# A two-layer graph network on one core: zeroing beside the sort, the search in the sort's buffers, layer norm beside the gathers

## The chip, the cores and the metric

The kernel runs on one core of a Trainium2 chip. The metric is the device time of one execution in microseconds (us). Engines are named as in the profile: PE (TensorE; PEld its weight loads), DVE (VectorE), ACT (ScalarE), POOL (GpSimd) and SP (SyncE). SP and ACT issue hardware DMAs, POOL issues the indirect ones (gathers by an index table).

## The reference

```python
h = jnp.maximum(_layernorm(x), 0.0)            # x: 12500 nodes x 48
x = x + _L0_gnn_ref(h, edge_index, W, b)       # edge_index = [src, dst], 400000 edges, dst sorted
h = jnp.maximum(_layernorm(x), 0.0)
x = x + _L1_gnn_ref(h, edge_index, edge_attr_16, W1, b1, W2, b2, W3, b3)
```

`_L0` adds up, for each `src` node, the rows of its `dst` nodes, scaled by the degrees, and multiplies by a 48 x 48 matrix. `_L1` runs a three-layer perceptron (112 to 128 to 128 to 48) over every edge, averages the messages by `dst` node and adds them to `x`.

## The kernel before, in words

There are three stages. The **preparation** (up to L642) brings the edge lists into the form that layer 0 needs. **Layer 0** (L645 to L852) works on it with one-hot matmuls. **Layer 1** (L906 to L1000) gathers one 128-edge tile after the other (L937) and runs the perceptron on it; its result is added into two tables `utab` in HBM, which must have been zeroed before. Only the preparation is changed.

The preparation runs in this order of the source:

- L106 loads the `dst` list as 71 partitions of 22,528 bytes (`raw`), L155 loads `x`, L160 to L177 the weights and biases. SP and ACT share them.
- L223 to L230 reduce `raw` to a maximum per 128 edges and put it into a table `rtab`; L252 reads it back for all partitions into `ka`. From it, 112 partitions each look for their own stretch of 4096 edges and gather it (L264, L277, L287: `mix_i`, `run_i`).
- L306 to L312 reduce `raw` to `lim` and write a table `wtab`. L314 to L330 turn `raw` into edge-major form: ACT converts (L322, `rawf`), PE transposes (L329), ACT evicts (L330). This is done for `dst` (into `rel`) and then, with a second load (L317), for `src` (into `src_i`).
- L286 to L301 make one sort key for each edge. L332 to L354 are a bitonic sort of 4096 keys in each of 112 partitions: 78 stages of two or four DVE instructions that go from buffer `ka` to `kb` and back. L356 writes the sorted keys to HBM (`ltab`), L357 keeps a sample of every 64th.
- L359 zeroes `utab`: a memset of `zero` (L198) and 14 DMAs of 128 x 1806 floats on SP's queue (L203).
- L400 to L412 search the sample for the place of 50 limits in each run (`coarse`, `where_i`). L414 gathers, for each limit, the 64 keys around it (`fine`, 50 gathers on POOL). L418 to L451 read `wtab` back (`wb2`, `top2`) and use it.
- L460 to L474 are the first layer norm and the 48 x 48 product: `norm_relu` (L362 to L383) in two halves, then 25 blocks of up to four tiles. For each block PE transposes (L468, `tp`), ACT evicts (L470), PE multiplies (L473, `lin`), ACT evicts (L474).
- L476 to L492 count in `fine`, give the exact slots, and end in the flag `good`, for which PE does one small matmul (L490, `w_ps`). Every engine reads `good` and branches on it (L642, L645).

Layer 0 then begins with 49 gathers of sorted keys (`slots`, L656); PE transposes them four at a time (L664), DVE and ACT work on them (L666 to L718).

The order in which an engine meets its instructions is not that of the source: a scheduler of the framework orders all instructions by its own estimate, and puts a wait where a buffer is written or read. Within one engine the order is then fixed. Buffers come from pools that are opened and closed like a stack; a tile in space that an earlier pool used waits for whoever used it last. DMAs of SP and ACT take eight hardware semaphores in turn, and a DMA waits until the one eight places before it has landed.

Of the kernel before, what the change touches and what calls it, by code (L numbers as in the profile page):

```python
# [15 lines left out]
P = 128  # L16
# [4 lines left out]
def kernel(  # L21
# [45 lines left out]
    B = 4  # L67
# [34 lines left out]

    early = ExitStack()
# [90 lines left out]
    def clear(tables, w, engines):  # L194

        with tc.tile_pool(name="zero", bufs=1) as zp:
            zero = zp.tile([P, ZH * w], FP, name="zero")
            nc.vector.memset(zero, 0.0)  # L198
            for k, t in enumerate(tables):
                v = t.rearrange("(p h) f -> p (h f)", p=P)  # L200
                n, m = v.shape[1], ZH * w
                for a in range(0, n, m):
                    engines[k % len(engines)].dma_start(  # L203
                        v[:, a : min(a + m, n)], zero[:, : min(m, n - a)]
                    )
# [32 lines left out]
    with tc.tile_pool(name="runs", bufs=1) as rp, tc.tile_pool(  # L238
        name="runs_ps", bufs=2, space=bass.MemoryType.PSUM
    ) as eps:  # L240
        iota_si = rp.tile([P, S], I32, name="iota_si")
        nc.gpsimd.iota(iota_si, pattern=[[1, S]], base=0, channel_multiplier=0)
        nc.vector.tensor_copy(iota_s, iota_si)
        run_i = rp.tile([ND, RUN], I32, name="run_i")
        nc.gpsimd.iota(run_i, pattern=[[1, RUN]], base=0, channel_multiplier=0)
        at = rp.tile([ND, RUN], FP, name="at")
        nc.vector.tensor_copy(at, run_i)
        ka = rp.tile([ND, RUN + P], FP, name="ka")
        kb = rp.tile([ND, RUN], FP, name="kb")
        nc.vector.memset(ka[:, RUN:], BIG)  # L250
        rmax, below = ka[:, :NT], kb[:, :NT]
        nc.sync.dma_start(rmax, rtab[0:1, :].to_broadcast([ND, NT]))  # L252
        ends2 = rp.tile([ND, 2], FP, name="ends2")
        for k in range(2):
            lim = rp.tile([ND, 1], FP, name=f"lim{k}")
            nc.vector.tensor_scalar(lim, first, float(k * D), None, op0=OP.add)
            nc.vector.tensor_scalar(below, rmax, lim, None, op0=OP.is_lt)
            whole = rp.tile([ND, 1], FP, name=f"whole{k}")
            nc.vector.tensor_reduce(whole, below, AX.X, OP.add)
            nc.vector.tensor_scalar(whole, whole, float(NT - 1), None, op0=OP.min)  # L260
            whole_i = rp.tile([ND, 1], I32, name=f"whole_i{k}")
            nc.vector.tensor_copy(whole_i, whole)
            mix_i = rp.tile([ND, P], I32, name=f"mix_i{k}")
            gather(mix_i, dst.rearrange("(t p) -> t p", p=P), whole_i)  # L264
            mix_f = rp.tile([ND, P], FP, name=f"mix_f{k}")
            nc.vector.tensor_copy(mix_f, mix_i)
            nc.vector.tensor_scalar(mix_f, mix_f, lim, None, op0=OP.is_lt)
            part = rp.tile([ND, 1], FP, name=f"part{k}")
            nc.vector.tensor_reduce(part, mix_f, AX.X, OP.add)
            nc.vector.scalar_tensor_tensor(  # L270
                ends2[:, k : k + 1], whole, float(P), part, op0=OP.mult, op1=OP.add
            )
        base = rp.tile([ND, 1], FP, name="base")
        nc.vector.tensor_scalar(base, ends2[:, 0:1], float(E - RUN), None, op0=OP.min)
        base_i = rp.tile([ND, 1], I32, name="base_i")
        nc.vector.tensor_copy(base_i, base)
        gather(run_i, dst.rearrange("(e o) -> e o", o=1), base_i)  # L277
        offs = rp.tile([ND, 2], FP, name="offs")
        nc.vector.tensor_scalar(offs, ends2, base, None, op0=OP.subtract)


        nc.vector.tensor_scalar(kb, at, offs[:, 0:1], None, op0=OP.is_ge)
        nc.vector.scalar_tensor_tensor(at, at, offs[:, 1:2], kb, op0=OP.is_lt, op1=OP.mult)
        inside = at
        sa, sb = ka[:, :RUN], kb
        nc.vector.tensor_scalar(sa, run_i, first, None, op0=OP.subtract)  # L286
        gather(run_i, src.rearrange("(e o) -> e o", o=1), base_i)  # L287
        nc.vector.tensor_tensor(kb, sa, inside, OP.mult)
        nc.vector.tensor_reduce(wrong[:, 0:1], kb, AX.X, OP.max)
        nc.vector.tensor_scalar(  # L290
            wrong[:, 0:1], wrong[:, 0:1], D - 0.5, None, op0=OP.is_gt
        )
        nc.vector.tensor_reduce(wrong[:, 1:2], kb, AX.X, OP.min)
        nc.vector.tensor_scalar(wrong[:, 1:2], wrong[:, 1:2], -0.5, None, op0=OP.is_lt)
        nc.vector.tensor_scalar(wrong[:, 2:3], offs[:, 1:2], RUN + 0.5, None, op0=OP.is_gt)
        nc.vector.tensor_tensor(wrong[:, 3:4], offs[:, 0:1], offs[:, 1:2], OP.is_gt)
        nc.vector.scalar_tensor_tensor(sa, run_i, float(P), sa, op0=OP.mult, op1=OP.add)
        nc.vector.scalar_tensor_tensor(
            sa, sa, BIG, inside, op0=OP.subtract, op1=OP.mult
        )  # L300
        nc.vector.tensor_scalar(sa, sa, BIG, None, op0=OP.add)  # L301


        lim = ep.tile([CP, 2, CC], FP, name="lim")
        flat = raw_d.rearrange("p (c e) -> p c e", c=CC)
        nc.vector.tensor_reduce(lim[:, 0], flat, AX.X, OP.min)  # L306
        nc.vector.tensor_reduce(lim[:, 1], flat, AX.X, OP.max)
        for k in range(2):
            nc.sync.dma_start(
                wtab[k, :NCH].rearrange("(p c) -> p c", p=CP), lim[:, k]  # L310
            )
            nc.sync.dma_start(wtab[k : k + 1, NCH:], lim1[:, k : k + 1])  # L312
        raw = raw_d
        for k, o in ((1, rel), (0, src_i)):  # L314
            if k == 0:
                raw = ep.tile([CP, CC * B * P], I32, name="raw")
                nc.sync.dma_start(raw, src[:E4].rearrange("(p e) -> p e", p=CP))  # L317
            nc.scalar.activation(o[:, NCH * B :], last_i[:, k : k + 1], AF.Copy)
            ov = o[:, : NCH * B].rearrange("p (q c b) -> p c q b", q=CP, b=B)
            for c in range(CC):  # L320
                rawf = ep.tile([CP, P, B], FP, name="rawf", bufs=3)
                nc.scalar.activation(  # L322
                    rawf,
                    raw.rearrange("p (c i j) -> p c i j", c=CC, j=B)[:, c],
                    AF.Copy,
                )
                tp = eps.tile([P, B, CP], FP, name="tp")
                for b in range(B):
                    nc.tensor.transpose(tp[:, b, :], rawf[:, :, b], ident[:CP, :CP])  # L329
                nc.scalar.activation(ov[:, c], tp.rearrange("p b q -> p q b"), AF.Copy)  # L330

        k = 2  # L332
        while k <= RUN:
            j = k // 2
            while j >= 1:
                if k < RUN:
                    a = sa.rearrange("p (n d m h j) -> p n d m h j", d=2, m=k // (2 * j), h=2, j=j)
                    b = sb.rearrange("p (n d m h j) -> p n d m h j", d=2, m=k // (2 * j), h=2, j=j)
                    ways = [(a[:, :, d], b[:, :, d], d) for d in range(2)]
                else:  # L340
                    a = sa.rearrange("p (n m h j) -> p n m h j", n=1, h=2, j=j)
                    b = sb.rearrange("p (n m h j) -> p n m h j", n=1, h=2, j=j)
                    ways = [(a, b, 0)]
                for a, b, d in ways:
                    for h in range(2):
                        nc.vector.tensor_tensor(  # L346
                            b[:, :, :, h],
                            a[:, :, :, 0],
                            a[:, :, :, 1],
                            OP.max if h != d else OP.min,  # L350
                        )
                sa, sb = sb, sa
                j //= 2
            k *= 2  # L354
        assert sa.offset == ka.offset
        nc.sync.dma_start(ltab, ka)  # L356
        nc.vector.tensor_copy(sample, sa.rearrange("p (i k) -> p i k", k=SK)[:, :, 0])  # L357
# [38 lines left out]
    with tc.tile_pool(name="begin", bufs=1) as bp_, tc.tile_pool(  # L396
# [59 lines left out]
        with tc.tile_pool(name="ln0", bufs=2) as lp, tc.tile_pool(  # L456
# [5 lines left out]
            for h0 in range(0, NH, HC):  # L462
                at_once(norm_relu(lp, h0, h0 + HC))
# [674 lines left out]
```

## Time and profile before

| | us |
|---|---|
| median of 4 runs (lowest to highest) | 6191.4 (6187.16 to 6197.04) |
| the profiled execution, its own time | 6189.63 |
| its span, first to last instruction | 6187.9 |
| DVE from the first to the last stage of the sort | 204.64 to 564.28 |
| flag `good` written (L492, start) | 692.91 |
| first gather of layer 0 (L656, `slots`) | 694.99 |

All starts are counted from the first instruction of the span. A row of the timeline reads: start, duration, engine, line, operation, written tile, read tiles, shape, count, and in brackets the idle time before it with what ended it. "SPq" and "ACTq" are the queues' DMA issues: the duration is that of the issue and not of the transfer. A row of the waits reads: who waited on whose instruction, us in total, times, longest.

### The profile page before, as it was taken

The numbers are of one execution on the slowest core, as the hardware profiler recorded it, in microseconds if no ns is written. First come the engines' busy times: TensorE is split into PE (matmuls) and PEld (weight loads), VectorE is DVE, ScalarE is ACT, GpSimd is POOL, SyncE is SP. The second block draws the span as 40 slices with busy tenths as digits, with TensorE's granted clock in tenths as the row PEclk, the third lists the DMA queues.
The fourth block names the chain that finished last, engine by engine and source line by source line (L and its number), as shares of the span: only waits on it lengthen the run. The fifth ranks groups of instructions, "written<-read, shape, count | busy, mean of one in ns | idle before, by whom it ended". The sixth has DMA issues, their size and how long they took to land.

```text
span 6187.9 us, 97254 instructions
## 1 busy us (share of the span) xinstructions
PE 4425.6 (72%) x35368; PEld 3350.1 (54%) x35368; DVE 3163.4 (51%) x4843; ACT 2302.3 (37%) x4904; POOL 3179.9 (51%) x3239
## 2 busy tenths in 40 slices
PE   0001559999999777777777777777777777777776
PEld 0001449999999555555455555455555555555555
DVE  3898489999999433333333333333333333333333
ACT  0001228888888422232223232333323223223331
POOL 0000700000000577777777777777777777777771
PEclk9999869999999899999999999999999999999996
DMA  2002134455444222222222222222222222222224
GB/s 69 3 0 99 31 82 149 146 148 146 147 147 144 63 48 47 47 44 48 48 46 48 44 48 46 48 44 48 48 46 47 45 48 46 47 44 48 46 40 105
DMA packets 397108, 407.58 MB, mean 66 GB/s; under 512 B 227482, under 2 KB 350958, under 8 KB 392111
## 3 DMA queue, kind: packets, MB, share of 16 engines
q1 hardware_dynamic: 155238, 273.99, 15.9%
q0 software_dynamic: 103488, 85.03, 10.1%
q10 hardware_dynamic: 137894, 42.24, 2.9%
q8 instruction: 283, 4.64, 0.3%
q14 instruction: 205, 1.67, 0.1%
HBM read 362.97 MB, written 38.02 MB: 65 GB/s over the span
## 4 chain that ended last, share of the span: by engine, by line
DMA 29%; PE 21%; POOL 17%; DVE 14%; issue 10%; ACT 6%; another core or an unknown queue 2%; POOLq 0%; ACTq 0%; DVEq 0%
DMA et<-htab,src_i 29%; POOL et L208 16%; PE u_ps L990 6%; ACT rows L797 5%; PE h_ps L970 3%; PE sum L809 3%; DVE kb L346 3%; DVE ka L346 3%; PE et_ps L953 2%; DVE ohs L781 2%; PE at_ps L793 2%; PE h_ps L959 2%; DVE oht L777 1%; DVE ohr L695 1%
## 5 line engine op out<-in xcount | busy, mean ns | idle before, releaser
L208 POOL DMA_INDIRECT et<-htab,src_i x3125 | 3055.6, 978 | 2230.6 <-PE tb L636 1277.4
L953 PE MATMUL et_ps<-ident,et 128*64 128x128 f32 x3125 | 686.1, 287 | 948.6 <-DMA et<-htab,src_i 936.2
L953 PEld LDWEIGHTS et_ps<-ident,et 128*64 128x64 f32 x3125 | 347.5, 111 | 1673.6 <-DMA et<-htab,src_i 985.8
L963 ACT ACTIVATE h<-h_ps,b_sb 128x512 f32<-128x512 f32 x782 | 537.7, 688 | 1623.7 <-PE h_ps L959 1623.7
L809 PE MATMUL sum<-rows,ohs 128*128 128x144 bf16 x10976 | 1008.8, 228 | 20.3 <-ACT rows L797 17.3
L797 ACT ACTIVATE rows<-at_ps 128x432 bf16<-128x432 f32 x1830 | 955.3, 531 | 142.9 <-DVE g L756 35.1
L974 DVE MEMSET h<- 128x4 f32 x782 | 48.5, 62 | 1844.4 <-PE u_ps L990 1844.4
L970 PE MATMUL h_ps<-w_sb,h 128*128 128x128 f32 x6250 | 990.0, 306 | 0.5 <-ACT h L963 0.5
L970 PEld LDWEIGHTS h_ps<-w_sb,h 128*128 128x128 f32 x6250 | 835.6, 208 | 170.8 <-ACT et L934 131.6
L990 PE MATMUL u_ps<-h,oh 128*40 128x129 f32 x6250 | 915.8, 292 | 0.0
L809 PEld LDWEIGHTS <-ohs 128*128 128x128 bf16 x10976 | 855.8, 144 | 25.7 <-issue 19.4
L975 DVE TENSOR_TENSOR h<-h_ps,b_neg 128x512 f32<-128x512 f32 x782 | 540.4, 691 | 594.5 <-PE h_ps L970 594.5
L959 PE MATMUL h_ps<-mv,wk 104*128 104x512 f32 x1564 | 828.3, 612 | 0.0
L954 ACT ACTIVATE mv<-et_ps 64x512 f32<-64x512 f32 x782 | 460.0, 588 | 988.6 <-PE et_ps L953 987.8
L781 DVE TENSOR_TENSOR ohs<-lo_b,iota_x 128x4096 bf16<-128x4096 bf16 (+1 forms) x350 | 786.0, 2246 | 51.1 <-PE sum L809 32.8
L990 PEld LDWEIGHTS u_ps<-h,oh 128*40 128x40 f32 x6250 | 679.8, 122 | 122.6 <-issue 33.2
L793 PE MATMUL at_ps<-g,oht 112*128 112x144 bf16 x5488 | 651.3, 226 | 35.9 <-DVE oht L777 35.5
L596 DVE TENSOR_SCALAR mv<-db,wid 40x512 f32<-40x512 int32 x782 | 534.1, 683 | 185.0 <-PE h_ps L959 174.6
L793 PEld LDWEIGHTS <-oht 112*128 112x128 bf16 x5488 | 416.2, 98 | 38.9 <-issue 35.9
L468 PE MATMUL tp<-ident,ht 128*48 128x128 f32 x98 | 25.7, 415 | 415.1 <-ACT ht L383 415.1
L208 POOL DMA_INDIRECT fine<-ltab,where_i x50 | 46.7, 934 | 506.3 <-ACT h_t L470 491.4
L941 DVE TENSOR_TENSOR oh<-rel,iota_f 128x160 f32<-128x160 f32 x782 | 255.7, 327 | 13.3 <-DMA wk<-in_L_gnn_W_dram 2.8
(190 smaller groups left out, 2382.3 us busy)
## 6 DMA issues: line engine op xcount, KB each, us to landing
at<-dltab SPq DMA_DIRECT2D x343, 448.0 KB
db<-in_dst_dram SPq DMA_DIRECT2D x97, 640.0 KB
et<-htab,src_i POOLq DMA_INDIRECT x3125, 2.5
ea<-in_edge_attr_dram ACTq DMA_DIRECT2D x97, 256.0 KB
utab<-zero SPq DMA_DIRECT2D x14, 903.0 KB
utab<-u SPq DMA_DIRECT2D x391, 20.2 KB
wk<-btab SPq DMA_DIRECT2D x391, 20.0 KB
uk<-utab SPq DMA_DIRECT2D x7, 903.0 KB
```

Source lines behind the costliest of these rows:

```text
L208: nc.gpsimd.indirect_dma_start(out=into, out_offset=None, in_=table, in_offset=bass.IndirectOffsetOnAxis(ap=idx, axis=0),)
L596: nc.vector.tensor_scalar(to.rearrange("p (j i) -> p j i", j=n), db[p0 : p0 + W, a : a + n * P].rearrange("p (i j) -> p j i", j=n), wid[p0 ...
L781: nc.vector.tensor_tensor(ohs[:, :n], lo_b[:, h0 : h0 + n, None, c : c + CG].to_broadcast([P, n, S, CG]), iota_x[:, None].to_broadcast([P, ...
L793: nc.tensor.matmul(ps3[:, i, :], oht[:, k, c % CG, :], g3[:, c, :], start=True, stop=True)
L797: nc.scalar.activation(rows[:, : len(tiles)], ps3[:, : len(tiles)], AF.Copy)
L809: nc.tensor.matmul(sums[k][:, j, :], ohs[:, k, j * P : (j + 1) * P, c % CG], rows[:, i, :], start=(c == 0 and j == 0), stop=(c == ND - 1 a ...
L953: nc.tensor.transpose(et_ps[:, j * P : (j + 1) * P], et[:, j, :], ident)
L959: nc.tensor.matmul(h1_ps[:, : n * P], k["wc"], k["mv"][:, : n * P], start=True, stop=True)
L963: nc.scalar.activation(h1[:, : n * P], h1_ps[:, : n * P], AF.Relu, bias=b1_sb)
L970: nc.tensor.matmul(h2_ps[:, j, :], h1[:, j * P : (j + 1) * P], w2_sb, start=True, stop=True)
L975: nc.vector.tensor_tensor(h2[:, :n, :H], h2_ps[:, :n], b2_neg[:, None, :].to_broadcast([P, n, H]), OP.max,)
L990: nc.tensor.matmul(u_ps, oh[:, j, :], h2[:, j, :], start=(q == 0 and j == 0), stop=(q == Q - 1 and j == n - 1),)
```

## The change

The sort's pool (`runs`) is opened earlier and stays open until `good` is written, so that its buffers can be used again. `clear` takes a pool from outside and is called before the sort in the source. `coarse` and `fine` become one view of the sort's buffer `at`; `wb2` and `top2` become views of `ka`; the layer norm's work space becomes the two halves of `kb`, which for that is declared as 128 x 2 x 2499 floats, of which the sort uses the first 4096 of 112 partitions. No operation is added or left out.

```diff
+    cut = ExitStack()
+    rp = cut.enter_context(tc.tile_pool(name="cuts", bufs=1))
+    where_i = rp.tile([ND, 2, NS + 1], I32, name="where_i")
+    sorting = ExitStack()
+    rp = sorting.enter_context(tc.tile_pool(name="runs", bufs=1))
     early = ExitStack()
...
-    def clear(tables, w, engines):
+    def clear(tables, w, engines, pool):
-        with tc.tile_pool(name="zero", bufs=1) as zp:
-            zero = zp.tile([P, ZH * w], FP, name="zero")
+        zero = pool.tile([P, ZH * w], FP, name="zero")
...
-        ka = rp.tile([ND, RUN + P], FP, name="ka")
-        kb = rp.tile([ND, RUN], FP, name="kb")
+    ka_all = rp.tile([P, RUN + P], FP, name="ka")
+    ka = ka_all[:ND]
+    HC = NH // 2
+    kb_all = rp.tile([P, 2, (F + 3) * HC], FP, name="kb")
+    kb = kb_all[:ND].rearrange("p k n -> p (k n)")[:, :RUN]
...
+    clear(utab, H1, (nc.sync, nc.sync), rp)
+
         k = 2
         while k <= RUN:
...
-    clear(utab, H1, (nc.sync, nc.sync))
     early.close()
-    def norm_relu(pool, h0, h1):
+    def norm_relu(pool, h0, h1, space=None):
+        if space is None:
             st = pool.tile([P, 3, n], FP, name="st")
             sq = pool.tile([P, n, F], FP, name="sq")
+        else:
+            st = space[:, : 3 * n].rearrange("p (k n) -> p k n", k=3)
+            sq = space[:, 3 * n :].rearrange("p (n f) -> p n f", f=F)
...
-        coarse = bp_.tile([ND, NS1, NK], FP, name="coarse")
+        coarse = fine = at[:, : NS1 * NK].rearrange("p (h k) -> p h k", k=NK)
...
-        fine = bp_.tile([ND, NS1, SK], FP, name="fine")
...
-        wb2 = bp_.tile([P, NG, Q], FP, name="wb2")
+        wb2 = ka_all[:, :NC1].rearrange("p (g q) -> p g q", q=Q)
...
-        top2 = bp_.tile([1, NG, Q], FP, name="top2")
+        top2 = ka_all[:1, NC1 : 2 * NC1].rearrange("p (g q) -> p g q", q=Q)
...
-            for h0 in range(0, NH, HC):
-                at_once(norm_relu(lp, h0, h0 + HC))
+            for k in range(2):
+                at_once(norm_relu(lp, k * HC, (k + 1) * HC, kb_all[:, k]))
...
+    sorting.close()
```

More of the change, by code (lines that the diff above doesn't have):

```diff
@@ L192 @@
     ZH = 14
-    def clear(tables, w, engines):
-        with tc.tile_pool(name="zero", bufs=1) as zp:
-            zero = zp.tile([P, ZH * w], FP, name="zero")
[L198 to L205, printed above, removed]
+    def clear(tables, w, engines, pool):
+        zero = pool.tile([P, ZH * w], FP, name="zero")
+        nc.vector.memset(zero, 0.0)
+        for k, t in enumerate(tables):
+            v = t.rearrange("(p h) f -> p (h f)", p=P)
+            n, m = v.shape[1], ZH * w
+            for a in range(0, n, m):
+                engines[k % len(engines)].dma_start(
+                    v[:, a : min(a + m, n)], zero[:, : min(m, n - a)]
+                )
     def gather(into, table, idx):
@@ L237 @@
     wrong = const.tile([ND, 5], FP, name="wrong")
[L238 to L247, printed above, removed]
-        ka = rp.tile([ND, RUN + P], FP, name="ka")
-        kb = rp.tile([ND, RUN], FP, name="kb")
[L250 to L271, printed above, removed]
-            )
[L273 to L357, printed above, removed]
@@ L359 @@
-    clear(utab, H1, (nc.sync, nc.sync))
+    eps = early.enter_context(tc.tile_pool(name="runs_ps", bufs=2, space=bass.MemoryType.PSUM))
+    iota_si = rp.tile([P, S], I32, name="iota_si")
+    nc.gpsimd.iota(iota_si, pattern=[[1, S]], base=0, channel_multiplier=0)
+    nc.vector.tensor_copy(iota_s, iota_si)
+    run_i = rp.tile([ND, RUN], I32, name="run_i")
+    nc.gpsimd.iota(run_i, pattern=[[1, RUN]], base=0, channel_multiplier=0)
+    at = rp.tile([ND, RUN], FP, name="at")
+    nc.vector.tensor_copy(at, run_i)
@@ new lines @@
+    ka_all = rp.tile([P, RUN + P], FP, name="ka")
[3 more added lines that the diff above has]
+    kb = kb_all[:ND].rearrange("p k n -> p (k n)")[:, :RUN]
+    nc.vector.memset(ka[:, RUN:], BIG)
+    rmax, below = ka[:, :NT], kb[:, :NT]
+    nc.sync.dma_start(rmax, rtab[0:1, :].to_broadcast([ND, NT]))
+    ends2 = rp.tile([ND, 2], FP, name="ends2")
+    for k in range(2):
+        lim = rp.tile([ND, 1], FP, name=f"lim{k}")
+        nc.vector.tensor_scalar(lim, first, float(k * D), None, op0=OP.add)
+        nc.vector.tensor_scalar(below, rmax, lim, None, op0=OP.is_lt)
+        whole = rp.tile([ND, 1], FP, name=f"whole{k}")
+        nc.vector.tensor_reduce(whole, below, AX.X, OP.add)
+        nc.vector.tensor_scalar(whole, whole, float(NT - 1), None, op0=OP.min)
+        whole_i = rp.tile([ND, 1], I32, name=f"whole_i{k}")
+        nc.vector.tensor_copy(whole_i, whole)
+        mix_i = rp.tile([ND, P], I32, name=f"mix_i{k}")
+        gather(mix_i, dst.rearrange("(t p) -> t p", p=P), whole_i)
+        mix_f = rp.tile([ND, P], FP, name=f"mix_f{k}")
+        nc.vector.tensor_copy(mix_f, mix_i)
+        nc.vector.tensor_scalar(mix_f, mix_f, lim, None, op0=OP.is_lt)
+        part = rp.tile([ND, 1], FP, name=f"part{k}")
+        nc.vector.tensor_reduce(part, mix_f, AX.X, OP.add)
+        nc.vector.scalar_tensor_tensor(
+            ends2[:, k : k + 1], whole, float(P), part, op0=OP.mult, op1=OP.add
+        )
@@ new lines @@
+    base = rp.tile([ND, 1], FP, name="base")
+    nc.vector.tensor_scalar(base, ends2[:, 0:1], float(E - RUN), None, op0=OP.min)
+    base_i = rp.tile([ND, 1], I32, name="base_i")
+    nc.vector.tensor_copy(base_i, base)
+    gather(run_i, dst.rearrange("(e o) -> e o", o=1), base_i)
+    offs = rp.tile([ND, 2], FP, name="offs")
+    nc.vector.tensor_scalar(offs, ends2, base, None, op0=OP.subtract)
+    nc.vector.tensor_scalar(kb, at, offs[:, 0:1], None, op0=OP.is_ge)
+    nc.vector.scalar_tensor_tensor(at, at, offs[:, 1:2], kb, op0=OP.is_lt, op1=OP.mult)
@@ new lines @@
+    inside = at
+    sa, sb = ka[:, :RUN], kb
+    nc.vector.tensor_scalar(sa, run_i, first, None, op0=OP.subtract)
+    gather(run_i, src.rearrange("(e o) -> e o", o=1), base_i)
+    nc.vector.tensor_tensor(kb, sa, inside, OP.mult)
+    nc.vector.tensor_reduce(wrong[:, 0:1], kb, AX.X, OP.max)
+    nc.vector.tensor_scalar(
+        wrong[:, 0:1], wrong[:, 0:1], D - 0.5, None, op0=OP.is_gt
+    )
+    nc.vector.tensor_reduce(wrong[:, 1:2], kb, AX.X, OP.min)
+    nc.vector.tensor_scalar(wrong[:, 1:2], wrong[:, 1:2], -0.5, None, op0=OP.is_lt)
@@ new lines @@
+    nc.vector.tensor_scalar(wrong[:, 2:3], offs[:, 1:2], RUN + 0.5, None, op0=OP.is_gt)
+    nc.vector.tensor_tensor(wrong[:, 3:4], offs[:, 0:1], offs[:, 1:2], OP.is_gt)
+    nc.vector.scalar_tensor_tensor(sa, run_i, float(P), sa, op0=OP.mult, op1=OP.add)
+    nc.vector.scalar_tensor_tensor(
+        sa, sa, BIG, inside, op0=OP.subtract, op1=OP.mult
+    )
+    nc.vector.tensor_scalar(sa, sa, BIG, None, op0=OP.add)
+    lim = ep.tile([CP, 2, CC], FP, name="lim")
+    flat = raw_d.rearrange("p (c e) -> p c e", c=CC)
@@ new lines @@
+    nc.vector.tensor_reduce(lim[:, 0], flat, AX.X, OP.min)
+    nc.vector.tensor_reduce(lim[:, 1], flat, AX.X, OP.max)
+    for k in range(2):
+        nc.sync.dma_start(
+            wtab[k, :NCH].rearrange("(p c) -> p c", p=CP), lim[:, k]
+        )
+        nc.sync.dma_start(wtab[k : k + 1, NCH:], lim1[:, k : k + 1])
+    raw = raw_d
+    for k, o in ((1, rel), (0, src_i)):
+        if k == 0:
+            raw = ep.tile([CP, CC * B * P], I32, name="raw")
+            nc.sync.dma_start(raw, src[:E4].rearrange("(p e) -> p e", p=CP))
+        nc.scalar.activation(o[:, NCH * B :], last_i[:, k : k + 1], AF.Copy)
+        ov = o[:, : NCH * B].rearrange("p (q c b) -> p c q b", q=CP, b=B)
+        for c in range(CC):
+            rawf = ep.tile([CP, P, B], FP, name="rawf", bufs=3)
+            nc.scalar.activation(
+                rawf,
+                raw.rearrange("p (c i j) -> p c i j", c=CC, j=B)[:, c],
+                AF.Copy,
+            )
+            tp = eps.tile([P, B, CP], FP, name="tp")
+            for b in range(B):
+                nc.tensor.transpose(tp[:, b, :], rawf[:, :, b], ident[:CP, :CP])
+            nc.scalar.activation(ov[:, c], tp.rearrange("p b q -> p q b"), AF.Copy)
@@ new lines @@
+    clear(utab, H1, (nc.sync, nc.sync), rp)
+    k = 2
+    while k <= RUN:
+        j = k // 2
+        while j >= 1:
+            if k < RUN:
+                a = sa.rearrange("p (n d m h j) -> p n d m h j", d=2, m=k // (2 * j), h=2, j=j)
+                b = sb.rearrange("p (n d m h j) -> p n d m h j", d=2, m=k // (2 * j), h=2, j=j)
+                ways = [(a[:, :, d], b[:, :, d], d) for d in range(2)]
+            else:
+                a = sa.rearrange("p (n m h j) -> p n m h j", n=1, h=2, j=j)
+                b = sb.rearrange("p (n m h j) -> p n m h j", n=1, h=2, j=j)
+                ways = [(a, b, 0)]
+            for a, b, d in ways:
+                for h in range(2):
+                    nc.vector.tensor_tensor(
+                        b[:, :, :, h],
+                        a[:, :, :, 0],
+                        a[:, :, :, 1],
+                        OP.max if h != d else OP.min,
+                    )
+            sa, sb = sb, sa
+            j //= 2
+        k *= 2
@@ L360 @@
+    assert sa.offset == ka.offset
+    nc.sync.dma_start(ltab, ka)
+    nc.vector.tensor_copy(sample, sa.rearrange("p (i k) -> p i k", k=SK)[:, :, 0])
     early.close()
-    def norm_relu(pool, h0, h1):
+    def norm_relu(pool, h0, h1, space=None):
         n = h1 - h0
         xs, hs = xt[:, h0:h1, :], ht[:, h0:h1, :]
-        st = pool.tile([P, 3, n], FP, name="st")
-        sq = pool.tile([P, n, F], FP, name="sq")
+        if space is None:
+            st = pool.tile([P, 3, n], FP, name="st")
+            sq = pool.tile([P, n, F], FP, name="sq")
+        else:
+            st = space[:, : 3 * n].rearrange("p (k n) -> p k n", k=3)
+            sq = space[:, 3 * n :].rearrange("p (n f) -> p n f", f=F)
@@ L387, in at_once @@
             pass
-    cut = ExitStack()
-    rp = cut.enter_context(tc.tile_pool(name="cuts", bufs=1))
     lflat = ltab.rearrange("p e -> (p e)").rearrange("(e o) -> e o", o=1)
@@ L394 @@
     NS1 = NS + 1
-    where_i = rp.tile([ND, 2, NS1], I32, name="where_i")
     with tc.tile_pool(name="begin", bufs=1) as bp_, tc.tile_pool(
@@ L451 @@
         nc.vector.tensor_reduce(worst, bad.rearrange("p a b -> p (a b)"), AX.X, OP.max)
-        HC = NH // 2
         w0_t = const.tile([F, F], FP, name="w0_t")
@@ L461 @@
             nc.vector.tensor_copy(w0_t, wt_ps)
-            for h0 in range(0, NH, HC):
-                at_once(norm_relu(lp, h0, h0 + HC))
+            for k in range(2):
+                at_once(norm_relu(lp, k * HC, (k + 1) * HC, kb_all[:, k]))
             for h0 in range(0, NH, B):
@@ L880 @@
         scaled()
-        clear([acc0], F, (nc.sync,))
-        clear([acc1], F1, (nc.sync,))
+        with tc.tile_pool(name="zero", bufs=1) as zp:
+            clear([acc0], F, (nc.sync,), zp)
+        with tc.tile_pool(name="zero", bufs=1) as zp:
+            clear([acc1], F1, (nc.sync,), zp)
         with tc.tile_pool(name="s0", bufs=2) as wp, tc.tile_pool(
```

## The prediction

> **What bounds the kernel now.** I read first the program's order on each engine before and after the change, with what each instruction waits for, to find how far the change reaches. From the first gather of layer 0 (`slots`) on, every engine has the same instructions in the same order, with the same waits, DMA semaphores and buffer addresses. So only the preparation counts, the first 695 us of the span, and there the time from its start to the first `slots` gather. The costliest group of the whole page (3125 gathers in layer 1) is out of reach.
>
> The preparation has three parts with different bounds. Ahead of the sort, the waits between 60 and 210 us show (who waited on whom: total, times, longest):
>
> ```profile
> ACT rawf L322 <- DMA raw<-in_src_dram: 79.3, 1, 79.3
> DVE w_t L461 <- PE wt_ps L460: 51.8, 1, 51.8
> ```
>
> ACT waits 79.3 us for the `src` list, a load of 71 long partitions. PE transposes it, and `wt_ps` (L460) stands behind those transposes on PE; DVE waits 51.8 us for it and only then starts the sort. So the landing of the `src` list starts the sort, and everything else ahead of it has about 50 us of slack. In the sort DVE is alone and its instructions follow each other; it bounds itself. Behind the sort, the waits between 560 and 700 us:
>
> ```profile
> DVE fine L476 <- DMA fine<-ltab,where_i: 60.4, 1, 60.4
> ...
> PEld w_ps L490 <- DVE wsum L488: 25.7, 1, 25.7
> PE w_ps L490 <- DVE wsum L488: 25.6, 1, 25.6
> ...
> DVE coarse L400 <- DMA utab<-zero: 11.9, 1, 11.9
> ...
> DVE zero L198 <- DMA ltab<-ka: 8.1, 1, 8.1
> ```
>
> DVE waits for `ltab`, zeroes, does layer norm, waits 11.9 us for the zero DMAs, searches `coarse`, and waits 60.4 us for 50 gathers. PE and ACT have long finished the layer norm's product and wait 25.6 us for the flag. The chain is the search. The timeline, row by row (start, duration; S is the start of `sample`, 564.2):
>
> ```profile
> 564.19 0.22 DVE L357 COPY sample<-ka 112x64 f32<-112x64 f32 x1
> ...
> 620.89 0.94 POOL L208 DMA_INDIRECT fine<-ltab,where_i  x1 [491.42 <-ACT h_t L470]
> ...
> 684.30 3.49 DVE L476 TENSOR_TENSOR fine<-fine,bound_all 112x3200 f32<-112x3200 f32 x1 [60.44 <-DMA fine<-ltab,where_i]
> ...
> 692.51 0.19 PE L490 MATMUL w_ps<-one_col,wsum 112*1 112x1 f32 x2 [25.58 <-DVE wsum L488]
> ...
> 694.99 0.93 POOL L208 DMA_INDIRECT slots<-ltab,where_i  x1 [12.46 <-issue]
> ```
>
> First search gather at S+56.7, last at S+117.4 (681.60, 49 steps of 1.239), count at S+120.1, flag matmul at S+128.3, first `slots` gather at S+130.8.
>
> **1. The zeroes ahead of the sort.** SP's issues before:
>
> ```profile
> 75.76 0.22 SPq L224 DMA_DIRECT2D rtab<-rows  x1
> 78.32 0.31 SPq L252 DMA_DIRECT2D ka<-rtab  x1
> 83.89 6.28 SPq L309 DMA_DIRECT2D wtab<-lim  x2
> 90.22 0.40 SPq L317 DMA_DIRECT2D raw<-in_src_dram  x1
> ...
> 564.30 0.31 SPq L356 DMA_DIRECT2D ltab<-ka  x1
> 574.12 16.05 SPq L203 DMA_DIRECT2D utab<-zero  x14
> ```
>
> The new order puts the 14 zero DMAs on this queue so: two ahead of `rtab<-rows`, one ahead of `ka<-rtab`, two between the `wtab` writes, seven right behind the load of the `src` list, two behind that load's landing. Each is spread over 16 DMA engines, 8 packets of about 0.28 us on each, so about 2.25 us. The first two delay `rtab` and `ka`, but those end in slack. What counts is the issue of the `src` load: it waits for ACT's last conversion of the `dst` list, and ACT's chain now begins later, because an ACT bias load (L182) takes the semaphore of the second zero DMA and waits until it landed: xt lands at 75.7, zeroes one and two follow, about 82.3, where ACT's conversions began at 79.86. With the table load behind it they begin 4.3 us later, less what ACT waited for anyway, so SP issues the load about 3.1 us later (93.3). All the list's packets ran on one DMA engine; zeroes four and five use it until about 96, hardly longer. Landing +3.2. DVE's extra work between landing and sort (`bad` memset 0.71, small ones) adds 0.6. **Sum +3.8.** The lower bound is that 0.6. The upper bound takes the seven zeroes issued behind the list as sharing its DMA engine: 7 x 8 x 0.28 = 15.7 more, +19.5. For the low side: in the trace, packets of `w0`, `w1b`, `w2`, `w3` queued on the engine that carried the `dst` list moved only after its end (65 to 75 us), and SP's issue at L166 took 12.87 us meanwhile. So a long load that is already running is not held up by later ones. I stay by that row.
>
> **2. The sort.** Its 288 DVE instructions stay. But `kb` is now a view into a three-dimensional tile, and the program's listing shows 102 of them with a semaphore wait on the instruction directly ahead; before there are 32. In the trace of before, 1024-wide instructions with such a wait start 1.251 us after their predecessor (18 cases), without it 1.136 (240 cases); the 2048-wide ones 2.319 against 2.209.
>
> ```profile
> 212.44 4.63 DVE L346 TENSOR_TENSOR ka<-kb 112x1024 f32<-112x1024 f32 x4
> 216.99 4.63 DVE L346 TENSOR_TENSOR kb<-ka 112x1024 f32<-112x1024 f32 x4
> 221.65 4.63 DVE L346 TENSOR_TENSOR ka<-kb 112x1024 f32<-112x1024 f32 x4
> ```
>
> Rows of four start 4.55 to 4.66 apart, three short steps and sometimes a long one. So 70 new waits x 0.115 = **+8.0**. Lower bound 0 (the wait may stand in what the 18 cases have otherwise in common, the turn of a stage), upper 8.0 again, since no case is dearer.
>
> The Trainium skill, "VectorE: DVE Perf Modes", section "The DRAIN you can't avoid", speaks against this term: eight copies in a row took the same 13.88 us with a semaphore after each. By that rule this term is 0 and the sum below is -4.9; the trace's 0.115 is the nearer row.
>
> **3. The search moved up.** With the zeroes gone and `coarse` in `at`, DVE goes on at S with the first layer norm reduction, then `coarse` and `where_i`, which ends at S+14.4 by its rows of before. The `wtab` read into `ka` (`wb2`) must wait for `ltab`'s landing, S+8.3, plus 3.6 of its own, S+12.0: just in time. The first search gather follows 1.1 later, S+15.5 (before: S+56.7), the last at S+76.2, count at S+78.9 (+2.70), flag matmul ready at S+87.1 (+8.20). The whole search is 41 us earlier.
>
> **4. What is late next.** The layer norm now runs beside the gathers, S+19.8 to S+37; then PE's chain of 25 blocks starts, where it began at S+31.0 before (595.19) and took until 667.22, 72 us. In the new order the flag's matmul `w_ps` no longer stands last on PE: it stands after 14 blocks transposed and 12 products. PE reaches it at S+37+37.2 = S+74 and waits there until S+87.3, some 13 us; behind it wait the rest of the blocks, and with them ACT, whose evictions are of these blocks. The rest took 34.6 us before (632.36 to 666.93):
>
> ```profile
> 632.36 1.94 PE L473 MATMUL lin<-w_t,h_t 48*128 48x48 f32 x8
> ```
>
> So layer 0 begins at S+87.3+34.7 = S+122, as its first `slots` gather waits for PE's last product and ACT's last `h_t`, against S+130.8: **-8.7**. So of the 41 us won, 32 go into the product chain with the pause in it.
>
> Bounds. High: if layer norm beside the gathers stretches them. Rows in layer 1: gathers beside fp32 tensor_tensor (L975, L941) last 0.944 and 0.953, alone 0.932 to 0.944, beside tensor_scalar (L596) 1.070, beside bf16 tensor_tensor (L695) 1.589. Layer norm takes some 17 us beside the gathers; eight gathers x 0.66 = 5.3 later, -3.4. Low: in the 35 us from 632 to 667 PE was busy for 34.40, its weight loads for 27.84; if after the pause only the loads bound it, because blocks lie ready, the rest takes 27.8 instead of 34.7: -15.6. I stay at -8.7, since the f32 rows are nearest to the gathers' case and PE was full without ACT holding it (0.5 us of idle time).
>
> The Trainium skill, "SBUF — State Buffer", section "Who interferes with whom", says that tensor_tensor leaves descriptor generation alone, while copies, casts and tensor_scalar can stall it; the rows above agree in direction, with a smaller amount (1.070).
>
> **The sum.** 3.8 + 8.0 - 8.7 = +3.1. The profiled execution took 6189.63, so 6192.7 by its own time; it is 1.8 under the median of the runs (6191.4), and on the median the forecast is **6194.5**. This is within 0.2% (12.4 us), about what a measurement of this kernel can tell from no change.
>
> **Rivals.**
> *Slower: the `src` list shares its DMA engine* with the seven zero DMAs queued behind it. Its place is the 79 us landing that starts the sort, its price up to 15.7: 3.1 + 15.7 = +18.8, 6210. It decides as soon as these zeroes cost it more than 9 us. For it: the zeroes have packets on that engine; against: the `dst` list was not held up so.
> *The sort's waits are free.* 3.8 - 8.7 = -4.9: 6186.5. For it: the 18 cases are few; against: the 1.251 shows at two widths.
> *The search gathers stretch* beside layer norm: 3.1 + 5.3 = +8.4, 6199.8.
> *Faster: free waits, an unpaced PE and the low bound of the preparation* together: 0.6 + 0 - 15.6 = -15.0, 6176.
> That the change doesn't do what it says, that the search stays behind the zeroes, is excluded by the listing of the order.
>
> **How the numbers follow.** Forecast 0.56, slower rival 0.20, free waits 0.10, stretched gathers 0.06, faster rival 0.08. Forecast, free waits and stretched gathers lie within 0.2%: 0.72; faster 0.08, slower 0.20. The range reaches from 6183, a bit under the free waits, to 6210, the slower rival with its bound.
>
> **What would show it.** In the changed profile: SP's issue of the `src` list at about 93 and its landing at about 172.6 (later by 9 or more: the slower rival). From the first sort stage to `sample` 367.6 instead of 359.6 (unchanged: the free waits). First search gather 15.5 after `sample`. PE waiting some 13 us for `w_ps` amid its blocks. First `slots` gather at 122 after `sample`: later by 5, stretched gathers; earlier by 7, unpaced PE. The forecast is wrong if the main loops differ from before at all, since nothing in their order does.

## The result, and the profile after

The changed kernel took 6201.8 us in the median (6193.34 to 6209.22, 31 runs), the kernel before 6189.76 (6179.56 to 6199.37, 51 runs): 1.0019 times as long, 95% interval 1.0014 to 1.0024, or 12 us more. The forecast was 3.1 us more, 6194.5. The profiled execution's span went from 6187.9 to 6202.5 us.

The preparation carries it. Layer 0's first gather starts at 708.18 us instead of 694.99, 13.2 later; from there to the end the two profiles differ by 1.4.

| us | before | after | change | forecast |
|---|---|---|---|---|
| first stage of the sort starts | 204.64 | 208.72 | +4.1 | +3.8 |
| from there to `sample` | 359.55 | 368.26 | +8.7 | +8.0 |
| from `sample` to the first `slots` gather | 130.8 | 131.2 | +0.4 | -8.7 |

The first two rows came close to the forecast; the third did not. The timeline of the changed kernel ahead of the sort, with SP's and ACT's DMA issues and ACT's first instructions behind the waits:

```profile
75.61 0.84 SPq L207 DMA_DIRECT2D utab<-zero  x2
...
80.43 0.33 SPq L207 DMA_DIRECT2D utab<-zero  x1
82.74 0.33 ACTq L182 DMA_DIRECT2D b_sb<-in_L_gnn_b_dram  x1
83.10 1.28 ACT L323 ACT_TABLE_LOAD   x1 [80.77 <-DMA utab<-zero]
...
93.55 0.26 SPq L322 DMA_DIRECT2D raw<-in_src_dram  x1
...
173.55 1.67 ACT L327 ACTIVATE rawf<-raw 71x512 f32<-71x512 int32 x3 [78.78 <-DMA raw<-in_src_dram]
```

ACT's bias load (L182) stands until 82.74, when the second zero DMA has landed; the table load and the conversions follow it, and the load of the `src` list goes out at 93.55 instead of 90.22. ACT's first conversion of that list starts 80.00 us after this issue; before the change it was 79.25. From this conversion to the sort both kernels take 35.17 us. Behind the sort, the rows of DVE and POOL around the first search gathers:

```profile
591.45 3.39 DVE L435 TENSOR_TENSOR rel<-rel,wb 128x3120 f32<-128x3120 f32 x1
591.79 3.86 POOL L212 DMA_INDIRECT at<-ltab,where_i  x1 [460.09 <-DVE where_i L419]
...
596.66 2.59 DVE L380 TENSOR_TENSOR ht<-xt,kb 128x2352 f32<-128x2352 f32 x1
597.31 2.75 POOL L212 DMA_INDIRECT at<-ltab,where_i  x1 [0.30 <-issue]
...
600.25 2.61 DVE L380 TENSOR_TENSOR ht<-xt,kb 128x2352 f32<-128x2352 f32 x1
600.37 3.30 POOL L212 DMA_INDIRECT at<-ltab,where_i  x1 [0.30 <-issue]
602.78 5.11 DVE L385 TENSOR_REDUCE kb<-kb 128x49 f32<-128x2352 f32 x2
603.97 0.94 POOL L212 DMA_INDIRECT at<-ltab,where_i  x1 [0.30 <-issue]
...
608.99 5.09 DVE L390 TENSOR_TENSOR ht<-ht,kb 128x2352 f32<-128x2352 f32 x2
610.16 2.21 POOL L212 DMA_INDIRECT at<-ltab,where_i  x1 [0.30 <-issue]
612.68 2.21 POOL L212 DMA_INDIRECT at<-ltab,where_i  x1 [0.30 <-issue]
```

Five gathers begin while a large tensor_tensor runs, and each ends about 0.8 us after that instruction does; beside the reductions (L385) a gather takes 0.94. The five last 14.33 us together, where 4.65 was to be expected at 0.93 each. So the last search gather starts 85.2 us after `sample` instead of the 76.2 forecast, though the first one is early (14.8). The waits behind the sort, and the gather that begins layer 0:

```profile
DVE at L481 <- DMA at<-ltab,where_i: 50.7, 1, 50.7
POOL slots L212 <- ACT ht L479: 45.0, 1, 45.0
...
PE w_ps L495 <- DVE wsum L493: 22.0, 1, 22.0
```

```profile
708.18 0.93 POOL L212 DMA_INDIRECT slots<-ltab,where_i  x1 [45.05 <-ACT ht L479]
```

PE waits 22.0 us for the flag amid its blocks (forecast 13), and POOL waits for ACT's last eviction of that chain before it may begin layer 0.

### The profile page after: what moved, and what is told of

Same layout as the page of the kernel before. It is cut to its first block, busy times and chain, and to the rows that moved or that the text cites. A ratio compares the mean times of both kernels' runs of the same rounds, so it can differ in the third digit from the quotient of the medians.

```text
span 6202.5 us, 97245 instructions
## 1 busy us (share of the span) xinstructions
PE 4432.0 (71%) x35368; PEld 3352.7 (54%) x35368; DVE 3169.4 (51%) x4843; ACT 2297.5 (37%) x4904; POOL 3190.6 (51%) x3239
## 4 chain that ended last, share of the span: by engine, by line
DMA 29%; PE 21%; POOL 17%; DVE 14%; issue 10%; ACT 6%; another core or an unknown queue 2%; SPq 0%; POOLq 0%; DVEq 0%; ACTq 0%
DMA et<-htab,src_i 28%; POOL et L212 16%; PE u_ps L999 6%; ACT rows L804 5%; PE sum L816 3%; PE h_ps L979 3%; DVE kb L353 3%; DVE ka L353 3%; PE et_ps L962 3%; DVE ohs L788 2%; PE at_ps L800 2%; PE h_ps L968 2%; DVE oht L784 1%; DVE ohr L702 1%
## 5 line engine op out<-in xcount | busy, mean ns | idle before, releaser
L984 DVE TENSOR_TENSOR h<-h_ps,b_neg 128x512 f32<-128x512 f32 x782 | 540.4, 691 | 589.0 <-PE h_ps L979 589.0
L212 POOL DMA_INDIRECT at<-ltab,where_i x50 | 56.4, 1128 | 475.0 <-DVE where_i L419 460.1
L950 DVE TENSOR_TENSOR oh<-rel,iota_f 128x160 f32<-128x160 f32 x782 | 256.1, 328 | 13.4 <-DMA wk<-in_L_gnn_W_dram 2.8
```

Of the source, the lines that this page charges most:

```text
L212: nc.gpsimd.indirect_dma_start(out=into, out_offset=None, in_=table, in_offset=bass.IndirectOffsetOnAxis(ap=idx, axis=0),)
L984: nc.vector.tensor_tensor(h2[:, :n, :H], h2_ps[:, :n], b2_neg[:, None, :].to_broadcast([P, n, H]), OP.max,)
```

## The experiments

All durations in the preparation are read from each kernel's profile. The runs came in three sets, each from one chip. On the chip of the first set (`kb`, zeroes, flag last, first probe) the kernel before takes 6984.9 us; on that of the second set (flag last once more, second probe, four edits together, layer norm ahead of the sort) it takes 7076.4. The chip of the last set, with the changed kernel itself, is like that of the prediction (6186.6). Times are compared only with the kernel before on the same chip.

**kb a tile of its own.** `kb` is `[ND, RUN]` again; layer norm gets a tile `kc` and is held behind `sample` (part of the edit):

```diff
-    kb_all = rp.tile([P, 2, (F + 3) * HC], FP, name="kb")
-    kb = kb_all[:ND].rearrange("p k n -> p (k n)")[:, :RUN]
+    kb = rp.tile([ND, RUN], FP, name="kb")
+    kc = rp.tile([P, 2, (F + 3) * HC], FP, name="kc")
```

> The changed kernel, but the sort's buffer kb is again a tile of its own with rows of 4096 floats, and the layer norm gets a separate tile; the order of all instructions on all engines is that of the changed kernel, and only the waits on the instruction directly ahead fall from 102 to 32 in the sort. Theory (the waits cost 0.115 to 0.12 us each): first sort instruction to sample 359.6 us instead of 368.3, time 8.7 us under the changed kernel, about 6193. Rival (the sort is longer for another reason, such as traffic of the zeroing): it stays at 368 and the time does not move.

From the first stage to `sample` it took 359.5 us; the rival's 368 did not come. In the changed kernel's own trace 1024-wide instructions with a wait on the one ahead start 1.257 us after it (86 cases), without it 1.137 (172); for 2048-wide ones it is 2.322 against 2.209. Both kinds have the same `kb` there, so it is the wait and not the longer rows of the view. The time told nothing: it was 1.0014 of the kernel before (1.0000 to 1.0028), and behind the sort that chip behaves otherwise (below).

**All zeroes behind the list.**

```diff
-    clear(utab, H1, (nc.sync, nc.sync), rp)
+    with tc.issue_after(load.ins):
+        clear(utab, H1, (nc.sync, nc.sync), rp)
```

> The changed kernel, with all 14 zero DMAs issued behind the load of the src list on SP's queue. Theory (the first two zeroes hold up a bias load of ACT, and with it ACT's conversions, and with them the issue of the src load): the src load is issued at about 90.2 us as in the kernel before, its landing takes the same 79 us although now 14 instead of 9 zeroes stand behind it, the sort starts 3.3 us earlier, time about 3.3 us under the changed kernel, 6198.5. Rival (the zeroes share the DMA engine of the list): the landing takes up to 15 us longer than 79 and the time rises.

SP's timeline of this kernel:

```profile
90.10 0.40 SPq L322 DMA_DIRECT2D raw<-in_src_dram  x1
90.55 92.50 SPq L207 DMA_DIRECT2D utab<-zero  x14
```

The list goes out at 90.10 as before the change, ACT's first conversion follows 79.28 us later (79.25 before the change) with 14 zeroes behind the list, and the sort starts at 204.55. The slower rival of the prediction is out. The time was 0.9996 of the kernel before on that chip (0.9976 to 1.0015), which tells nothing.

**The flag's matmul last on PE.**

```diff
-                    nc.tensor.matmul(lin[:, j, :], h_t[:, j, :], w0_t, start=True, stop=True)
+                    mm = nc.tensor.matmul(lin[:, j, :], h_t[:, j, :], w0_t, start=True, stop=True)
...
-        nc.tensor.matmul(w_ps, wsum, one_col[:ND], start=True, stop=True)
+        with tc.issue_after(mm.ins):
+            nc.tensor.matmul(w_ps, wsum, one_col[:ND], start=True, stop=True)
```

> The changed kernel, with the flag's small matmul put behind the last product of the layer norm's chain on PE; nothing else moves. Theory (PE's pause of 22 us amid its blocks takes back what the earlier search won): no pause, the chain runs from 36.8 to about 109 us after sample, layer 0's first gather at about 111 instead of 131.2 after sample, time 20 us under the changed kernel, about 6182. Rival (something else of the longer search ends last, the pause is hidden): first gather stays near 131, no gain.

On that chip layer 0's first gather came 148.1 us after `sample`, which is neither theory's number, and the time was 1.0006 of the kernel before (0.9987 to 1.0026). ACT's evictions in PE's chain started up to 20.4 us late, while POOL issued its search gathers and some 8 us beyond, and not after that. The trace names no releaser for them that lies on the core. The same kernel was run on another chip:

> The changed kernel, with the flag's small matmul behind the last product of the layer norm's chain on PE, once more: in the first run ACT started its evictions up to 20 us late while the search gathers ran, as it does not in the changed kernel's own profile, so that it told nothing of the pause. Theory (PE's pause takes back what the earlier search won): where ACT is not held up, the chain runs without a pause, layer 0's first gather stands at about 111 us after sample instead of 131.2, 20 us under the changed kernel, a ratio of about 0.999 to the kernel before. Rival (ACT is held up by the gathers, pause or no pause): the gather stands at 131 or later, ratio 1.002 or more.

The gather came at 148.2 again, with a ratio of 0.9991 (0.9969 to 1.0012). So on these two chips nothing can be said of the pause. The last set had the changed kernel beside it:

> The changed kernel itself, unaltered, beside the three others. On a chip like that of its first profile: 12 us over the kernel before, first gather of layer 0 at 131 us after sample. On a chip where ACT starts its evictions late beside the search gathers: PE's chain is behind the flag's matmul anyway, the pause vanishes in ACT's lateness, and the gather stands at about 148 after sample, as in the kernel with the flag last.

> The flag's matmul behind the last product, now beside the changed kernel itself on one chip. Theory (PE's pause takes back what the earlier search won): where ACT is not late, layer 0's first gather at 111 instead of 131 us after sample and 20 us under the changed kernel; where ACT is late beside the gathers, the same time as the changed kernel within 3 us, because the pause lies beside ACT's lateness. Rival (the pause costs nothing anywhere): the same time on either chip.

There the changed kernel took 6198.08 us, 1.0016 of the kernel before (1.0007 to 1.0026), with layer 0's first gather 131.3 us after `sample`. With the flag last it took 6176.55, 0.9981 (0.9972 to 0.9990), with that gather at 111.2:

```profile
687.33 0.94 POOL L212 DMA_INDIRECT slots<-ltab,where_i  x1 [23.84 <-issue]
```

The gain is 20.1 us by the traces and 21.5 by the medians. The pause is what took back the earlier search.

**Which instructions hold a gather.** The first probe:

> The changed kernel with extra DVE instructions beside the search gathers, their results unused: after a reduction as a mark, two each of tensor_tensor (both operands in SBUF, no broadcast), tensor_scalar, scalar_tensor_tensor and copy on 128 x 2352 floats, and four tensor_tensor of 128 x 512 with one operand in PSUM, a reduction between the kinds. Theory (an instruction that reads two SBUF operands keeps the gather's descriptors from being written until it ends): gathers beside tensor_tensor and scalar_tensor_tensor last until some 0.8 us after its end, as the 2.2 to 3.9 us of the changed kernel; beside reductions 0.93; beside the operand in PSUM 0.93. tensor_scalar and copy between, up to 1.4 us. Rival (the gathers were long because of the broadcast operand, ACT or other traffic): tensor_tensor without broadcast leaves them at 0.93. The time itself rises by the stretch, some 5 to 15 us.

The scheduler put all the added instructions but the first reduction and one tensor_tensor behind the count; this tensor_tensor, without broadcast, lengthened its gather to 2.50. The second probe has them in place:

> The changed kernel with extra DVE instructions beside the search gathers, their results unused, this time all ahead of the count in fine (in the first probe all but one stood behind it): two each of tensor_tensor, tensor_scalar, scalar_tensor_tensor and copy on 128 x 2352 floats in SBUF, then four tensor_tensor of 128 x 512 with one operand in PSUM, a reduction between the kinds. Theory (an instruction that reads two SBUF operands keeps the gather from ending until some 0.8 us after it): gathers beside tensor_tensor and scalar_tensor_tensor 2.2 to 2.6 us, beside reductions and beside the operand in PSUM 0.93; beside tensor_scalar and copy (1.39 us each) up to 1.4 us or, if they hold it as long as they run, up to 2.2. Rival (only tensor_tensor does it): scalar_tensor_tensor, tensor_scalar and copy leave 0.93.

Its timeline shows gathers, in order, beside tensor_tensor, a reduction, tensor_scalar, scalar_tensor_tensor, copy, and tensor_tensor with an operand in PSUM:

```profile
615.46 2.61 DVE L491 TENSOR_TENSOR kb<-xt 128x2352 f32<-128x2352 f32 x1
616.37 2.50 POOL L212 DMA_INDIRECT at<-ltab,where_i  x1 [0.30 <-issue]
...
620.74 2.60 DVE L488 TENSOR_REDUCE kb<-xt 128x49 f32<-128x2352 f32 x1
621.82 0.94 POOL L212 DMA_INDIRECT at<-ltab,where_i  x1 [0.30 <-issue]
623.06 1.82 POOL L212 DMA_INDIRECT at<-ltab,where_i  x1 [0.30 <-issue]
623.38 1.38 DVE L494 TENSOR_SCALAR kb<-xt 128x2352 f32<-128x2352 f32 x1
...
628.86 2.61 DVE L497 SCALAR_TENSOR_TENSOR kb<-xt 128x2352 f32<-128x2352 f32 x1
629.78 2.50 POOL L212 DMA_INDIRECT at<-ltab,where_i  x1 [0.30 <-issue]
...
636.47 1.82 POOL L212 DMA_INDIRECT at<-ltab,where_i  x1 [0.31 <-issue]
636.78 1.39 DVE L500 COPY kb<-xt 128x2352 f32<-128x2352 f32 x1
...
642.26 2.87 DVE L504 TENSOR_TENSOR kb<-pp,kb 128x512 f32<-128x512 f32 x4
643.18 0.94 POOL L212 DMA_INDIRECT at<-ltab,where_i  x1 [0.31 <-issue]
```

All four forms that have all their tensors in SBUF hold gathers, the reduction excepted; a reduction and a tensor_tensor with one operand in PSUM do not (0.94). The six gathers that began inside one of the four forms ended 0.8 us after it: they took 2.50 and 2.34 beside tensor_tensor and scalar_tensor_tensor, 1.81 and 1.80 beside the second tensor_scalar and the second copy. Where the gather had begun 0.3 us ahead, the forms differ: tensor_scalar and copy still held it, until 0.1 us after their end (1.82), while tensor_tensor and scalar_tensor_tensor let it through (615.13 and 628.54, 0.94 each). Both rivals (broadcast; tensor_tensor alone) fall. Of each probe there is one execution, and its time is not used.

**Layer norm's small tile in PSUM.**

```diff
-            st = space[:, : 3 * n].rearrange("p (k n) -> p k n", k=3)
+            st = mean
...
+              mean = ps.tile([P, 3, HC], FP, name=f"mean{k}", bufs=1)
```

`ps` is a pool in PSUM; layer norm is also held behind `sample`.

> The changed kernel with the layer norm's small tile of means and factors in PSUM instead of SBUF, so that its large tensor_tensor read one operand from PSUM; the scheduler also moves the first of them ahead of where_i, so the search starts about 3 us later. Theory (two operands in SBUF hold the gathers): the gathers beside L380 and L390 last 0.93 instead of 2.2 to 3.3 us, only the one beside L435 stays long (3.9), and from the first to the last gather it is 64 us instead of 70.4. Rival (layer norm's size or ACT's part of it does it): still 2 to 3 us each.

```profile
601.09 2.60 DVE L390 TENSOR_TENSOR ht<-ht,mean 128x2352 f32<-128x2352 f32 x1
...
602.66 0.93 POOL L212 DMA_INDIRECT at<-ltab,where_i  x1 [0.30 <-issue]
```

This gather begins and ends while L390 runs. Only the gather beside L435 is long (4.19); beside L380 and L390 the gathers take 0.93 or 0.94, at the full size of layer norm's instructions. From the first to the last gather it is 64.0 us (70.4 in the changed kernel). The search started no later (14.5 after `sample`). One run took 6171.08 against 6186.6 for the kernel before; `w_ps` stands some blocks later in it and waits 9.7 instead of 22, so this gain is not the stretch alone.

**Versions faster than the kernel before.** First four edits together: those to `kb`, the zeroes and the flag, and DVE's search section held behind `sample`:

```diff
-    with tc.tile_pool(name="begin", bufs=1) as bp_, tc.tile_pool(
+    with tc.issue_after(took.ins), tc.tile_pool(name="begin", bufs=1) as bp_, tc.tile_pool(
```

> The changed kernel with four things mended: kb a tile of its own (no extra waits), the zeroes issued behind the src list, the flag's matmul last on PE, and DVE's part of the search section (row, bad, the copy w_t) issued behind sample, so that none of them stands between the key building and the sort. Theory (the src list starts the sort only because an instruction that waits for PE's transposes of it stands ahead of the sort on DVE): the sort starts at about 155 us instead of 208.7, takes 359.6, layer 0's first gather at about 111 after sample, or 131 to 145 where ACT is late beside the gathers: 50 to 70 us under the kernel before. Rival (the sort needs something else that lands with the src list): the sort starts at 204 and the gain is at most 20 us.

The sort started at 162.05 (204.55 with the zeroes alone moved): it does not need the load of the `src` list. The 7 us beyond the forecast are a second index gather's landing: DVE waits 9.45 us at L302 for `run_i`. That gather is stretched too: it runs beside the tensor_tensor L293, takes 5.00 us instead of 0.93, and ends 0.8 after L293. The ratio is 0.9903 (0.9873 to 0.9934), with layer 0's first gather at 151.9 after `sample` (forecast 131 to 145) on a chip where ACT is late. Then layer norm ahead of the sort (part of the edit):

```diff
+    for k in range(2):
+        at_once(norm_relu(None, k * HC, (k + 1) * HC, kc[:, k]))
     raw = raw_d
     for k, o in ((1, rel), (0, src_i)):
```

> As the kernel with four things mended, but with the layer norm ahead of the sort on DVE and its product chain on PE and ACT beside the sort, and the transpose of the weights ahead of those of the src list. Theory: layer norm costs DVE about 22 us ahead of the sort, part of them in its waits there, so that the sort starts at about 163; behind the sort only the search is left, with one gather stretched, and layer 0's first gather stands at 93 us after sample: 79 us under the kernel before (0.987), also where ACT is late beside gathers, because no eviction is left beside them. Rival (the sort is slowed by PE and ACT working beside it): the sort takes more than 360 us.

The ratio is 0.9827 (0.9810 to 0.9844) there; the sort takes 359.8 us, so PE and ACT beside it do not slow it. And beside the changed kernel:

> The best version once more, beside the changed kernel on one chip: in its first run the sort started at 180.5 us (204.6 before), took 359.8, and layer 0 began 87.5 us after sample, 67 us earlier than in the kernel before. Theory: that gain is there on either chip, 67 us or a ratio of 0.989, more where ACT is late beside gathers (0.983 in the first run). Rival (most of the first run's 118 us came from something else): a ratio under 0.985 also where ACT is not late.

It took 6118.09 us, 0.9886 of the kernel before (0.9871 to 0.9901): 68.5 us less, as the theory said; what the rest of the gain on the other chip came from is open, as the kernel before has no trace there. The sort starts at 180.78 (forecast 163: layer norm delays the index gathers, and DVE waits 13.55 us for `run_i`, whose gather lasts 4.76 beside L345 and L287), takes 359.85, and layer 0's first gather stands 87.5 after `sample`, at 628.12.

## Why the prediction was right or wrong

- **What bounds the preparation.** Right ahead of the sort, as a statement on both kernels' order. The four-edit version shows that it is the order of DVE's instructions and not the data that ties the sort to the list's load; the prediction saw `w_t` there and did not draw that.
- **1, zeroes.** The size was right, +4.1 for +3.8, and partly by luck. The list's issue moved by 3.3 (3.1 forecast), through ACT's late start. The 0.6 of extra DVE work did not come: it ran where DVE had waited for PE before (35.17 from conversion to sort in both). In its place the list took 0.75 longer from issue to first conversion; over the runs with this order that stretch spreads from 77.3 to 80.0. The row by which a running list is not held up was the true one: of each of the seven zero DMAs issued behind it, 120 of 128 packets moved while the list was under way, and the rest after its end.
- **2, the waits.** Right: +8.7 for +8.0; a wait costs 0.120 us on the 1024-wide instructions instead of 0.115. What "VectorE: DVE Perf Modes" of the Trainium skill, section "The DRAIN you can't avoid", found on eight copies, that a semaphore costs nothing extra, does not hold for these instructions.
- **3, the search.** The start was right (14.8 for 15.5 after `sample`), its length wrong (70.4 us from the first gather to the last instead of 60.7).
- **4, what is late next.** The mechanism was right: PE's pause amid its blocks, and 35.2 us from its end to layer 0 (34.7 forecast). The failed step is the sentence "I stay at -8.7, since the f32 rows are nearest to the gathers' case", which put the stretch of the search gathers at nothing. The stretch measured 9.7, above even the bound of 5.3; less the 0.7 of the earlier start, the last gather is 9.0 late, and the pause grew from 13 to 22 by the same 9. Those f32 rows misled: one (L941, L950 after) is over in 0.33 us, the other (L975, L984 after) reads an operand from PSUM, and neither holds a gather for long. The row set aside, the bf16 tensor_tensor L695 with 1.589 (it lies in layer 0 and not in layer 1), has both operands in SBUF and was the nearest. What counts is where the operands lie, and how much of the instruction is left when the gather begins. The bound failed as it priced a mean overhead for each gather from the bf16 row; the four gathers beside L380 and L390 lost 1.3 to 2.4 us each. It also left out L435 (3.39 us, search work), whose gather lost 2.9.
- The page "SBUF — State Buffer" of the Trainium skill, section "Who interferes with whom", was read for its inference that tensor_tensor leaves descriptor generation alone. As the prediction used it, the runs contradict it (2.2 to 3.9 us instead of 0.93), and the prediction's own row of 1.589 did not agree with it. Another sentence there, that a DVE instruction with two SBUF inputs contends with a GpSimd instruction that reads SBUF, agrees with the runs, if the gather's read of its index table counts as one. No run here tells which access is held.
- **The sum.** 4.1 + 8.7 + 0.4 = 13.2 in place of 3.1; of the 10 missing, 9.0 are the late last gather. The case "search gathers stretch" named the mechanism, at 8.4 and 6199.8. The measured 6201.8 lies beyond that case and still within the stated range, whose upper end of 6210 came from the slower rival. That rival did not occur, so this is luck.

## What to carry to other kernels

An indirect gather that begins while DVE runs an instruction with all its tensors in SBUF, reductions excepted, ended here about 0.8 us after that instruction. So hide PSUM-reading work or reductions under gathers, and price the rest at what is left of the instruction when the gather begins. A gather that begins just ahead is not safe either: one that began 0.07 us ahead of layer norm's last tensor_tensor pair took 0.93 in the changed kernel (608.92) and 3.40 in the four-edit version (554.30). When work is moved up, look in each engine's order for what now stands behind a late wait: here a one-column matmul cost 20 us. An idle stretch ahead of a long stage may be the order's doing: a few small instructions behind the wrong wait kept the sort some 40 us from starting.

## What had not been expected of the hardware

On the two chips of the first two sets, PE's mean granted clock was 0.85 over the run (0.94 on the chip of the last set), yet 1.00 in the preparation. There ACT's evictions beside gathers started up to 20 us late, which the chip of the last set did not show with the same kernel (flag last: 148 against 111 us). What holds ACT there stays open.
